# A decoder's expert choices put in ascending order, and part of the experts' outputs gathered during the last pairs of experts

## The chip, the cores and the metric

The kernel runs as one launch on one core of a Trainium2 chip. A core has five engines that run side by side, each with its own stream of instructions: TensorE (PE, matrix products; its weight loads are shown as PEld), VectorE (DVE), ScalarE (ACT), GpSimd (POOL) and SyncE (SP, which here only issues DMAs). They wait for one another by semaphores, and share 16 DMA engines. The metric is the device time of one execution in microseconds, lower is better. The kernel before takes 3460.56 us, the median of 3 runs (3460.08 to 3462.9).

## The reference, cut to what matters

A decoder of two layers works on `x` of 8 batches x 256 tokens x 512 features. Layer 0 has a windowed self-attention, a cross-attention with a layernorm on its result, and a mixture of 64 experts plus a shared expert; layer 1 a Mamba-2 block, a cross-attention and a second feed-forward. Each block's result is added to `x`. The change touches the mixture and its seam to Mamba:

```python
def _L0_ffn_ref(hidden_states, gate_weight, Wg, Wu, Wd, Sg, Su, Sd):
    ...
    logits = x.astype(jnp.float32) @ gate_weight.astype(jnp.float32).T
    scores = jax.nn.softmax(logits, axis=-1)
    group_scores = scores.reshape(T, NG, E // NG).max(axis=-1)
    _, gidx = jax.lax.top_k(group_scores, TG)
    ...
    tmp_scores = jnp.where(smask > 0, scores, 0.0)
    topk_w, topk_i = jax.lax.top_k(tmp_scores, K)
    ...
    slot = flat * C + jnp.minimum(pos, C - 1)
    ...
    out = jnp.einsum('ecm,ehm->ech', jax.nn.silu(g) * u, Wd).reshape(E * C, H)
    yk = out[slot].reshape(T, K, H)
    y = jnp.sum(yk * topk_w[..., None].astype(yk.dtype), axis=1)
    shared = jax.nn.silu(x @ Sg.T) * (x @ Su.T) @ Sd.T
    return (y + shared).reshape(B, S, H)
```

K is 6, E 64, and an expert has C = 192 slots. The sum over a token's six experts is the same in any order of the six, but for rounding. Mamba then reads the layernorm of the new `x`:

```python
    x = x + _L0_ffn_ref(_layernorm(x, axis=-1), L0_ffn_gate_weight, L0_ffn_Wg, L0_ffn_Wu, L0_ffn_Wd, L0_ffn_Sg, L0_ffn_Su, L0_ffn_Sd)
    x = x + _L1_attn_ref(_layernorm(x, axis=-1), L1_attn_in_proj_w, L1_attn_conv_w, L1_attn_conv_b, L1_attn_dt_bias, L1_attn_A_log, L1_attn_D, L1_attn_norm_w, L1_attn_out_proj_w)
```

## The kernel before

`x` stays in SBUF as 16 tiles x0 to x15 of 128 tokens x 512; batch b is x(2b) and x(2b+1). The stages follow one another: attention (0 to 560 us of the profile), cross-attention (560 to 1145), experts (1145 to 1950), Mamba (to about 2370), then the rest of layer 1. All matrix products go through `mm` (L100), all weight loads from DRAM through `load` (L103) and the SP queue into a ring of eight weight tiles `w`.

The cross-attention carries the front of the mixture along with it: in steps of a hand-written table, each batch also gets its layernorm, its routing, its slots, and the shared expert. `l0_choose` takes a batch's 2 x 64 logits per lane, softmaxes them (`sco`), keeps three of eight groups (`gm`), and takes the eight largest (MAX8, L892) with their indices (FIND_INDEX8, L893): weights to `topw`, indices to `topi`, largest weight first. `sel` marks the six chosen (MATCH_REPLACE8, L900). `slot` turns choices into rows of the experts' buffers: three operations on 768 elements (L767 equal, L771 times, L773 sum) pick the position of each choice, and `read[:, k, i]` keeps the row of choice k of x tile i. The shared expert is `hidden(b, m)` for six blocks m (eight matmuls into a PSUM bank, silu on ACT L843 into `act`, a product on DVE L844 into `hT`) and `down`. At the end of the stage a map from slots to tokens is read back from DRAM (L827, tiles `part0`, `part1`) and gives `slots`.

`l0_experts` runs 32 pairs of experts. Per pair POOL gathers three tiles `xg` of 128 rows from `xn_d` by `slots` (L916, an indirect DMA), PE transposes them (`turn`, L926), the copies make `xgT`; per expert three `hidden` steps follow (eight matmuls, silu on ACT L951, product on DVE L952 into `aT`), then `first` (128 of the 192 rows) and, once per pair, `last` (64 rows of both): their results go to the tile `yo` and by the SP queue to `y_d` in DRAM (L962, L977). `first` and `last` of a pair run one step late, `late` holding them.

Mamba starts from the combination of these outputs: `combine(pool, b)` gathers, for each of a batch's two tiles and each k, the rows `read[:, k, i]` of `y_d` into a tile `ye` (indirect DMA issued by POOL, L667, six buffers) and adds it times `topw` to x (DVE, L670). Each gather waits for every write to `y_d`. `normal(b)` is the layernorm of x (L161 to L169, its power on POOL, L153), `turn(b)` PE's transposes of it (L1040, ACT copies to `xnT`, L1041), `steps` and `convolve` the projections, `begin` and `scan` the recurrence in two halves (DVE's `dA` and `tri`, L1104; POOL's `xdt`, L1114), `result` the addition to x. The loop works in rounds: in round b, `turn` works on batch b+2, `normal` on b+3, `combine` on b+4, so four batches of `combine` stand in the program ahead of the first `begin`:

```python
                (turn, 2), (result, 0, 1), (normal, 3), (lambda b: combine(pool, b), 4),
            )
            for b in range(-4, B):
```

The order of instructions on an engine is set by a scheduler from its own estimates, except where `pin` keeps an instruction at its place in the program's order among other pinned ones; all of PE's are pinned, and `in_order` makes `layernorm` and `rsqrt` pin theirs. A pool's tile with a tag has `bufs` buffers (2 if nothing is said), which are handed out in turn; a tile waits until the last reader of the buffer's former tile is done.

Of the kernel before, what the change touches and what calls it, by code (L numbers as in the profile page):

```python
# [18 lines left out]
P = 128  # L19
# [23 lines left out]
    "ident": P, "lt": P, "gt": P, "le": P, "ones": P,  # L43
    "third": HC, "iota": E0, "base": E0,
}
# [23 lines left out]
class Decoder:  # L69
# [578 lines left out]
    def l0_moe(self, outer):  # L648


        nc, a = self.nc, self.a
        xn_d = self.dram.tile([T, D], F32, name="xn_d")
        y_d = self.dram.tile([NSLOT, D], F32, name="y_d")
        keep = outer.enter_context(self.pool("c0k", 1))
        topw = keep.tile([P, NT, 8], F32, name="topw")
        read = keep.tile([P, TOPK, NT], I32, name="read")
        slots = keep.tile([P, NSC], I32, name="slots")
        self.l0_cross(lambda *pools: self.l0_front(*pools, xn_d, topw, read, slots))
        with ExitStack() as ctx:
            self.ps = ctx.enter_context(self.psum("ps"))  # L660
            self.l0_experts(ctx.enter_context(self.pool("c2")), xn_d, slots, y_d)

        def combine(pool, b):
            for i in (2 * b, 2 * b + 1):
                for k in range(TOPK):
                    y = pool.tile([P, D], F32, tag="ye", name="ye", bufs=6)
                    nc.gpsimd.indirect_dma_start(  # L667
                        y, None, y_d, bass.IndirectOffsetOnAxis(ap=read[:, k, i : i + 1], axis=0)
                    )
                    nc.vector.scalar_tensor_tensor(  # L670
                        self.x[i], y, topw[:, i, k : k + 1], self.x[i], ALU.mult, ALU.add
                    )

        return combine

    def l0_front(self, one, pool, bank, xn_d, topw, read, slots):

# [21 lines left out]
        by_lane = lambda m: m.rearrange("(p i) o -> p (i o)", p=P)  # L699
        zero = one.tile([P, NSC], I32, name="zero")  # L700
        nc.vector.memset(zero, 0)
# [28 lines left out]
        def route(b):  # L730
            w = work[b]
            gate = self.small["gate"].rearrange("p (c e) -> p c e", c=HC)
            t = bank()
            lo = t[:, : 2 * E0].rearrange("p (i e) -> p i e", i=2)
            for i in range(2):
                for c in range(HC):
                    self.mm(lo[:, i, :], w["xnT"][:, c, i * P : (i + 1) * P], gate[:, c, :], c == 0, c == HC - 1)
            w["topi"] = topi = pool.tile([P, 2, 8], F32, tag="topi", name="topi")
            w["sel"] = self.l0_choose(pool, lo, topw[:, 2 * b : 2 * b + 2, :], topi)

        def slot(b):
# [11 lines left out]
            for i in range(2):  # L753
# [3 lines left out]
            nc.scalar.copy(pos, t[:, : 2 * E0].rearrange("p (i e) -> p i e", i=2))  # L757
            past = pool.tile([P, 2, E0], F32, tag="past", name="past", bufs=1)
            nc.vector.tensor_scalar(past, pos, CAP - 1.0, float(BAD), ALU.is_ge, ALU.mult)
# [8 lines left out]
                hit, self.iota.unsqueeze(1).unsqueeze(1).to_broadcast(every),  # L768
                w["topi"][:, :, :TOPK].unsqueeze(3).to_broadcast(every), ALU.is_equal,
            )  # L770
# [59 lines left out]
        def hidden(b, m):  # L830
            w = work[b]
            if m == 0:
                w["hT"] = pool.tile([P, n_m, S], F32, tag="hT", name="hT", bufs=1)
            n = rows(m)
            t = bank()
            for h, name in enumerate("gu"):
                for c in range(HC):
                    self.mm(
                        t[:n, h * S : (h + 1) * S], up[name][c // 2][:, c % 2, m * MB : m * MB + n],
                        w["xnT"][:, c, :], c == 0, c == HC - 1,  # L840
                    )
            act = pool.tile([P, S], F32, tag="act", name="act")
            nc.scalar.activation(act[:n], t[:n, :S], AF.Silu)  # L843
            self.pin(nc.vector.tensor_tensor(w["hT"][:n, m, :], act[:n], t[:n, S:], ALU.mult))  # L844
# [12 lines left out]

    def l0_choose(self, pool, logits, topw, topi):

# [35 lines left out]
        t8 = new("t8", 8)  # L895
        nc.vector.tensor_copy(t8, topw)
        nc.vector.memset(t8[:, :, TOPK:], -1.0)
        sel = new("sel", E0)
        for i in range(2):
            nc.vector.match_replace(sel[:, i, :], t8[:, i, :], tmp[:, i, :], -2.0)  # L900
        nc.vector.tensor_scalar(sel, sel, -1.5, None, ALU.is_lt)
        return sel

    def l0_experts(self, pool, xn_d, slots, y_d):

# [34 lines left out]
        def hidden(pair, h, m):  # L940
# [40 lines left out]
        for n in range(3):  # L981
            turn(0, n)
        late = []
        for pair in range(E0 // 2):
            for h in range(2):
                load(pair, h)
                for m in range(3):
                    if h == 0 and pair + 1 < E0 // 2:
                        gather(pair + 1, m)
                    hidden(pair, h, m)  # L990
                    if m == 0:
                        for work in late:
                            work()
                        late = []
                    if (h, m) in ((0, 2), (1, 1), (1, 2)) and pair + 1 < E0 // 2:
                        turn(pair + 1, m if h else 0)
                late = [lambda pair=pair, h=h: first(pair, h)]
                if h == 1:
                    late.append(lambda pair=pair: last(pair))
        for work in late:  # L1000
            work()


    def l1_mamba(self, combine):

# [12 lines left out]
        with ExitStack() as ctx:  # L1018
# [515 lines left out]
def decode(tc, a, out):  # L1534
    with ExitStack() as ctx:
        d = Decoder(ctx, tc, a, out)
        d.load_first()
        with ExitStack() as late:
            d.l0_attention()
            combine = d.l0_moe(late)  # L1540
            d.l1_mamba(combine)
        d.l1_cross()
# [3 lines left out]
def shape_constants():  # L1546
# [17 lines left out]
        "third": np.where(p % HD // 3 == np.arange(HC)[None, :], -1.0, 0.0),  # L1564
        "iota": row(np.arange(E0)), "base": row(np.arange(E0) * CAP),
        "mask": mask, "keep": keep,
# [73 lines left out]
```

## Time and profile before

| what | us |
|---|---|
| median of 3 runs | 3460.56 |
| profiled execution, its own time | 3465.64 |
| profiled execution, its span | 3463.9 |
| PE busy in the span | 3247.0 (94%) |
| DVE busy | 1598.5 (46%) |
| POOL busy | 758.5 (22%) |
| experts: 1145 to 1950, PE busy | 800.71 |
| seam: 1950 to 2000, PE busy | 12.16 |
| first rounds of Mamba: 2000 to 2100, PE busy | 76.09 |
| a steady batch of the cross stage: length, PE busy, DVE busy | 85.5, 82.0, 71.0 |

The profile is of one execution on the chip. Times are in us from the start of the span. A row of instructions gives the line of the kernel, the engine, the operation, the tile written and those read, and the number and length; "[28.60 <-DVE xn L169]" after a row of the timeline says that the engine idled 28.60 us before it, and what ended that. A row of windows gives each engine's busy time in that stretch with the number of its instructions, then the clock granted to TensorE as a share of full speed, the share in which the 16 DMA engines were busy, and the GB/s that they moved. Lengths on POOL are rough, and PE's ends are modelled.

### The profile page before, as it was taken

How to read it: one execution, taken by the hardware profiler on the slowest of the kernel's cores; microseconds unless marked ns; L12 is line 12 of the kernel's file. 1: busy time of each engine (PE TensorE's matmuls, PEld its weight loads, DVE VectorE, ACT ScalarE, POOL GpSimd, SP SyncE). 2: the span in 40 equal slices, each digit the busy share in tenths (PEclk: the TensorE clock that was granted, in tenths of full speed). 3: DMA queues.
4: the chain of work that ended last, by engine and by line, in shares of the span. 5: the costliest groups of instructions: out<-in, count | busy, mean ns of one | idle time of the engine just before them, and what ended most of it. 6: DMA issues, size and time to landing. Idle time of an engine off the chain costs nothing.

```text
span 3463.9 us, 47107 instructions
## 1 busy us (share of the span) xinstructions
PE 3247.0 (94%) x18803; PEld 2114.8 (61%) x18803; DVE 1598.5 (46%) x3784; ACT 998.6 (29%) x1959; POOL 758.5 (22%) x792
## 2 busy tenths in 40 slices
PE   7999878999999899999999578998999899999999
PEld 5666545666666687878787455563444566666665
DVE  4555589888875000000000288655666333333332
ACT  1222223333342122222222133442555322222221
POOL 3222001222235211111110276322121111111111
PEclk9999989999999999999999778997999899999999
DMA  4000010000100677777777743011000000000000
GB/s 175 1 1 1 7 64 16 13 13 13 35 7 21 198 234 236 237 236 242 232 245 224 223 140 91 1 33 50 26 26 17 34 7 6 7 7 1 7 6 13
DMA packets 106812, 272.57 MB, mean 79 GB/s; under 512 B 15136, under 2 KB 23968, under 8 KB 105696
## 3 DMA queue, kind: packets, MB, share of 16 engines
q1 hardware_dynamic: 88128, 219.16, 19.3%
q0 software_dynamic: 18464, 50.40, 5.2%
q8 instruction: 148, 2.42, 0.3%
q14 instruction: 72, 0.59, 0.1%
HBM read 235.81 MB, written 33.70 MB: 78 GB/s over the span
## 4 chain that ended last, share of the span: by engine, by line
PE 67%; DVE 12%; POOL 3%; issue 2%; DMA 2%; ACT 1%; SPq 0%; POOLq 0%; DVEq 0%; ACTq 0%
PE mm L100 18%; PE sc L100 15%; PE out L100 7%; PE w L100 6%; PE s L100 4%; PE a L100 3%; PE b L100 3%; PE sums L100 2%; PE acc L100 2%; PE st L100 2%; DVE e L526 1%; PE pt L926 1%; PE rt L100 1%; POOL ye L667 1%; DVE acc L1066 1%
## 5 line engine op out<-in xcount | busy, mean ns | idle before, releaser
L100 PE MATMUL sc<-xgT,w 128*112 128x192 f32 (+1 forms) x3072 | 529.6, 328 | 0.0
L100 PEld LDWEIGHTS sc<-xgT,w 128*112 128x112 f32 (+1 forms) x3072 | 497.4, 182 | 41.1 <-issue 40.9
L952 DVE TENSOR_TENSOR aT<-act,sc 112x192 f32<-112x192 f32 (+1 forms) x192 | 68.0, 354 | 741.3 <-ACT act L951 741.3
L100 PE MATMUL mm<-xnT,w 128*128 128x256 f32 x1152 | 280.9, 401 | 7.4 <-ACT xnT L252 5.9
L100 PE MATMUL mm<-w,aT 112*128 112x512 f32 (+3 forms) x768 | 262.7, 596 | 0.0
L100 PEld LDWEIGHTS mm<-xnT,w 128*128 128x128 f32 x1152 | 227.2, 201 | 46.2 <-ACT xnT L252 8.2
L100 PE MATMUL w<-xnT,w 128*128 128x256 f32 x1024 | 242.9, 380 | 0.0
L100 PE MATMUL out<-w,mix 128*128 128x512 f32 x512 | 240.4, 592 | 0.0
L1483 DVE TENSOR_TENSOR h<-base,b 128x512 f32<-128x512 f32 x128 | 88.0, 687 | 327.4 <-PE b L100 327.4
L916 POOL DMA_INDIRECT xg<-xn_d,slots x96 | 90.9, 947 | 641.2 <-PE pt L926 634.8
L100 PEld LDWEIGHTS w<-xnT,w 128*128 128x128 f32 x1024 | 192.2, 190 | 61.1 <-issue 40.7
L1487 POOL TENSOR_TENSOR mix<-h 128x256 f32<-128x256 f32 x128 | 93.1, 727 | 610.4 <-DVE h L1485 549.6
L1344 DVE TENSOR_REDUCE m<-s 128x1 f32<-128x512 f32 x256 | 164.6, 685 | 102.3 <-PE s L100 83.5
L153 POOL TENSOR_TENSOR lnr<-lne,c_nhalf 128x1 f32<-128x1 f32 x112 | 66.6, 596 | 645.7 <-DVE lne L151 639.5
L100 PE MATMUL st<-q,k 32*128 32x256 f32 (+1 forms) x1024 | 196.6, 545 | 1.2 <-ACT e L522 1.2
L100 PE MATMUL mm<-mT,w 128*118 128x256 f32 (+1 forms) x768 | 175.2, 388 | 9.8 <-DVE hT L844 9.8
L1293 ACT ACTIVATE e<-st 128x512 f32<-128x512 f32 x256 | 138.9, 595 | 141.9 <-PE st L100 140.2
L951 ACT ACTIVATE act<-sc 112x192 f32<-112x192 f32 (+1 forms) x192 | 63.6, 331 | 402.0 <-PE sc L100 402.0
L100 PEld LDWEIGHTS out<-w,mix 128*128 128x128 f32 x512 | 97.3, 190 | 122.4 <-issue 120.5
L100 PEld LDWEIGHTS mm<-w,aT 112*128 112x128 f32 (+3 forms) x768 | 95.6, 163 | 122.5 <-issue 122.5
L100 PEld LDWEIGHTS mm<-mT,w 128*118 128x118 f32 (+1 forms) x768 | 141.9, 186 | 45.9 <-DVE hT L844 12.1
L100 PE MATMUL s<-k,q 32*128 32x512 f32 x512 | 159.9, 700 | 6.3 <-issue 3.5
(333 smaller groups left out, 5315.1 us busy)
## 6 DMA issues: line engine op xcount, KB each, us to landing
w<-in_Wg SPq DMA_DIRECT2D x64, 704.0 KB, 7.7
w<-in_Wu SPq DMA_DIRECT2D x64, 704.0 KB, 4.6
w<-in_Wd SPq DMA_DIRECT2D x64, 448.0 KB, 6.4
w<-in_Wd SPq DMA_DIRECT2D x64, 256.0 KB, 5.4
y_d<-yo SPq DMA_DIRECT2D x64, 256.0 KB, 3.9
y_d<-yo SPq DMA_DIRECT2D x64, 128.0 KB, 4.1
w<-in_W SPq DMA_DIRECT2D x8, 1024.0 KB, 5.5
x<-in_x SPq DMA_DIRECT2D x16, 256.0 KB, 5.8
```

What stands on the lines that cost most here:

```text
L100: self.pin(self.nc.tensor.matmul(out, lhs, rhs, start=start, stop=stop))
L153: ins = nc.gpsimd.tensor_tensor(r, e, self.nhalf[:, :n], ALU.pow)
L526: self.pin(nc.vector.scalar_tensor_tensor(e, e, 1.0, low, ALU.max, ALU.mult))
L667: nc.gpsimd.indirect_dma_start(y, None, y_d, bass.IndirectOffsetOnAxis(ap=read[:, k, i : i + 1], axis=0))
L916: nc.gpsimd.indirect_dma_start(xg, None, xn_d, bass.IndirectOffsetOnAxis(ap=slots[:, i : i + 1], axis=0))
L926: self.pin(nc.tensor.transpose(t[:, blk], w[n][:, blk], self.ident))
L951: nc.scalar.activation(act[:n_m], ps[:n_m, :CAP], AF.Silu)
L952: nc.vector.tensor_tensor(w["a", h][:n_m, m, :], act[:n_m], ps[:n_m, S : S + CAP], ALU.mult)
L1293: nc.scalar.activation(w["e"][kc][:, j, :], st, AF.Exp, scale=SCALE)
L1344: nc.vector.tensor_reduce(m, sc, AX.X, ALU.max)
L1483: nc.vector.tensor_tensor(both(h), twice(base), both(t), ALU.add)
L1487: nc.gpsimd.tensor_tensor(mix, h[:, :G], h[:, G:], ALU.add)
```

## The change

1. `l0_choose` no longer keeps the largest first. The masked scores go to a tile `gates` (64 per token, kept until the experts are done), the six largest are found as before, `sel` marks them, and the marked indices are then sorted: `sel` times a constant 64 - e (`down`), the eight largest of that (MAX8), and 64 minus those are the indices in ascending order. FIND_INDEX8 and two copies go. So the k-th choice of a token has an index of at most 58 + k.
2. The weights in this order are taken later: `weigh(pool, b)`, three operations on 768 elements for each batch, in the first eight pairs of the experts' stage.
3. In the last two pairs `early` issues three gathers at every `hidden` step, of choices whose experts are all written: k = 0, 1 of x0 to x8 in pair 30, k = 2, 3 of the same tiles in pair 31, 36 of the 96. A gather reads from `known`, the first (59 + k) x 192 rows of `y_d`, and so waits for the writes to these alone. There are twelve buffers `ye` for them; the additions come three steps later, pinned on DVE, and what is left of them after the last pair. The products of `aT` (L952) are pinned too.
4. `combine` has the other 60: four in each of batches 0 to 3, eight in batch 4, twelve in each of batches 5 to 7. `normal(0)` is pinned; after it `hold` copies the indices of x0 to x5 on POOL, and the gathers of batches 1 and 2 read this copy, so they stay behind it.
5. To make room, `act` of the shared expert has one buffer for two, `past` shares a buffer with the scores, and the tile `zero` with `part0`.

In the order of instructions PE's stays as it was. On SP, the read of `part0` moves ahead of a 704 KB weight load at the start of the experts. On POOL, all `xg` gathers come ahead of all `ye` gathers. ACT has two table loads more, and one copy of `xgT` at the start of the experts goes from ACT to DVE.

```diff
@@ -652,28 +652,67 @@
         xn_d = self.dram.tile([T, D], F32, name="xn_d")
         y_d = self.dram.tile([NSLOT, D], F32, name="y_d")
         keep = outer.enter_context(self.pool("c0k", 1))
-        topw = keep.tile([P, NT, 8], F32, name="topw")
+        inner = ExitStack()
+        chosen = inner.enter_context(self.pool("c0g", 1))
+        gates = chosen.tile([P, NT, E0], F32, name="gates")
+        topi = chosen.tile([P, NT, 8], F32, name="topi")
+        topw = keep.tile([P, NT, TOPK], F32, name="topw")
         read = keep.tile([P, TOPK, NT], I32, name="read")
         slots = keep.tile([P, NSC], I32, name="slots")
-        self.l0_cross(lambda *pools: self.l0_front(*pools, xn_d, topw, read, slots))
+        self.l0_cross(lambda *pools: self.l0_front(*pools, xn_d, gates, topi, read, slots))
+
+        todo = [(i, k) for i in range(NT) for k in range(TOPK)]
+
+        def fetch(pool, i, k, bufs=6, at=read):
+            y = pool.tile([P, D], F32, tag="ye", name="ye", bufs=bufs)
+            known = y_d[: (E0 - TOPK + k + 1) * CAP, :]
+            nc.gpsimd.indirect_dma_start(
+                y, None, known, bass.IndirectOffsetOnAxis(ap=at[:, k, i : i + 1], axis=0)
+            )
+            return y
+
+        def add(i, k, y):
+            return nc.vector.scalar_tensor_tensor(self.x[i], y, topw[:, i, k : k + 1], self.x[i], ALU.mult, ALU.add)
+
+        def early(pool, done, n):
+
+            got = [(i, k) for i, k in todo if E0 - TOPK + k < done][:n]
+            for ik in got:
+                todo.remove(ik)
+            got = [(i, k, fetch(pool, i, k, 12)) for i, k in got]
+            return [lambda g=g: self.pin(add(*g)) for g in got]
+
+        def weigh(pool, b):
+
+            two = slice(2 * b, 2 * b + 2)
+            every = [P, 2, TOPK, E0]
+            hit = pool.tile(every, F32, tag="hit", name="hit", bufs=1)
+            nc.vector.tensor_tensor(
+                hit, self.iota.unsqueeze(1).unsqueeze(1).to_broadcast(every),
+                topi[:, two, :TOPK].unsqueeze(3).to_broadcast(every), ALU.is_equal,
+            )
+            nc.vector.tensor_tensor(hit, hit, gates[:, two, :].unsqueeze(2).to_broadcast(every), ALU.mult)
+            nc.vector.tensor_reduce(topw[:, two, :], hit, AX.X, ALU.add)
+
         with ExitStack() as ctx:
             self.ps = ctx.enter_context(self.psum("ps"))
-            self.l0_experts(ctx.enter_context(self.pool("c2")), xn_d, slots, y_d)
+            self.l0_experts(ctx.enter_context(self.pool("c2")), xn_d, slots, y_d, weigh, early)
+        inner.close()
+
+        held = []
+
+        def hold(pool):
+
+            held.append(pool.tile([P, TOPK, 6], I32, name="held"))
+            self.pin(nc.gpsimd.tensor_copy(held[0], read[:, :, :6]))
 
         def combine(pool, b):
-            for i in (2 * b, 2 * b + 1):
-                for k in range(TOPK):
-                    y = pool.tile([P, D], F32, tag="ye", name="ye", bufs=6)
-                    nc.gpsimd.indirect_dma_start(
-                        y, None, y_d, bass.IndirectOffsetOnAxis(ap=read[:, k, i : i + 1], axis=0)
-                    )
-                    nc.vector.scalar_tensor_tensor(
-                        self.x[i], y, topw[:, i, k : k + 1], self.x[i], ALU.mult, ALU.add
-                    )
-
-        return combine
-
-    def l0_front(self, one, pool, bank, xn_d, topw, read, slots):
+            for i, k in [t for t in todo if t[0] // 2 == b]:
+                add(i, k, fetch(pool, i, k, at=held[0] if held and b in (1, 2) else read))
+
+        return combine, hold
+
+    def l0_front(self, one, pool, bank, xn_d, gates, topi, read, slots):
 
 
         nc, a = self.nc, self.a
...
@@ -697,7 +736,7 @@
 
         maps = [self.dram.tile([NSLOT, 1], I32, name=f"map{k}_d") for k in range(2)]
         by_lane = lambda m: m.rearrange("(p i) o -> p (i o)", p=P)
-        zero = one.tile([P, NSC], I32, name="zero")
+        zero = pool.tile([P, NSC], I32, tag="part0", name="zero", bufs=1)
         nc.vector.memset(zero, 0)
         for m in maps:
             self.pin(nc.sync.dma_start(by_lane(m), zero))
...
@@ -755,7 +794,7 @@
                 nc.vector.tensor_tensor(cum, cum, sel, ALU.add)
                 nc.vector.scalar_tensor_tensor(late, sel, token[:, 2 * b + i : 2 * b + i + 1], late, ALU.mult, ALU.max)
             nc.scalar.copy(pos, t[:, : 2 * E0].rearrange("p (i e) -> p i e", i=2))
-            past = pool.tile([P, 2, E0], F32, tag="past", name="past", bufs=1)
+            past = pool.tile([P, 2, E0], F32, tag="sco", name="past", bufs=1)
             nc.vector.tensor_scalar(past, pos, CAP - 1.0, float(BAD), ALU.is_ge, ALU.mult)
             nc.vector.scalar_tensor_tensor(
                 pos, pos, CAP - 1.0, self.base.unsqueeze(1).to_broadcast([P, 2, E0]), ALU.min, ALU.add
...
@@ -839,7 +878,7 @@
                         t[:n, h * S : (h + 1) * S], up[name][c // 2][:, c % 2, m * MB : m * MB + n],
                         w["xnT"][:, c, :], c == 0, c == HC - 1,
                     )
-            act = pool.tile([P, S], F32, tag="act", name="act")
+            act = pool.tile([P, S], F32, tag="act", name="act", bufs=1)
             nc.scalar.activation(act[:n], t[:n, :S], AF.Silu)
             self.pin(nc.vector.tensor_tensor(w["hT"][:n, m, :], act[:n], t[:n, S:], ALU.mult))
 
...
@@ -883,25 +922,27 @@
         for i in range(2):
             nc.vector.match_replace(gm[:, i, :], g8[:, i, :], gs[:, i, :], -2.0)
         nc.vector.tensor_scalar(gm, gm, -1.5, None, ALU.is_lt)
-        tmp = new("tmp", E0)
         nc.vector.tensor_tensor(
-            groups(tmp), groups(sco), gm.unsqueeze(3).to_broadcast([P, 2, NG, E0 // NG]), ALU.mult
+            groups(gates), groups(sco), gm.unsqueeze(3).to_broadcast([P, 2, NG, E0 // NG]), ALU.mult
         )
-        ti = new("ti", 8, U32)
+        t8 = new("t8", 8)
         for i in range(2):
-            nc.vector.max(topw[:, i, :], tmp[:, i, :])
-            nc.vector.max_index(ti[:, i, :], topw[:, i, :], tmp[:, i, :])
-        nc.vector.tensor_copy(topi, ti)
-        t8 = new("t8", 8)
-        nc.vector.tensor_copy(t8, topw)
+            nc.vector.max(t8[:, i, :], gates[:, i, :])
         nc.vector.memset(t8[:, :, TOPK:], -1.0)
         sel = new("sel", E0)
         for i in range(2):
-            nc.vector.match_replace(sel[:, i, :], t8[:, i, :], tmp[:, i, :], -2.0)
+            nc.vector.match_replace(sel[:, i, :], t8[:, i, :], gates[:, i, :], -2.0)
         nc.vector.tensor_scalar(sel, sel, -1.5, None, ALU.is_lt)
+
+        order = new("sco", E0)
+        nc.vector.tensor_tensor(order, sel, self.down.unsqueeze(1).to_broadcast(wide), ALU.mult)
+        for i in range(2):
+            nc.vector.max(t8[:, i, :], order[:, i, :])
+        nc.vector.tensor_scalar(topi, t8, -1.0, float(E0), ALU.mult, ALU.add)
         return sel
 
-    def l0_experts(self, pool, xn_d, slots, y_d):
+    def l0_experts(self, pool, xn_d, slots, y_d, weigh, early):
+
 
 
         nc, a = self.nc, self.a
...
@@ -949,7 +990,7 @@
                     )
             act = pool.tile([P, CAP], F32, tag="act", name="act", bufs=3)
             nc.scalar.activation(act[:n_m], ps[:n_m, :CAP], AF.Silu)
-            nc.vector.tensor_tensor(w["a", h][:n_m, m, :], act[:n_m], ps[:n_m, S : S + CAP], ALU.mult)
+            self.pin(nc.vector.tensor_tensor(w["a", h][:n_m, m, :], act[:n_m], ps[:n_m, S : S + CAP], ALU.mult))
 
         def first(pair, h):
             w = state[pair]
...
@@ -980,8 +1021,10 @@
             gather(0, n)
         for n in range(3):
             turn(0, n)
-        late = []
+        late, adds, done = [], [], 0
         for pair in range(E0 // 2):
+            if pair < B:
+                weigh(pool, pair)
             for h in range(2):
                 load(pair, h)
                 for m in range(3):
...
@@ -992,16 +1035,22 @@
                         for work in late:
                             work()
                         late = []
+                        if h == 0:
+                            done = 2 * pair
+
+                    adds.append(early(pool, done, 3) if done >= E0 - 4 else [])
+                    for work in adds.pop(0) if len(adds) > 3 else []:
+                        work()
                     if (h, m) in ((0, 2), (1, 1), (1, 2)) and pair + 1 < E0 // 2:
                         turn(pair + 1, m if h else 0)
                 late = [lambda pair=pair, h=h: first(pair, h)]
                 if h == 1:
                     late.append(lambda pair=pair: last(pair))
-        for work in late:
+        for work in late + sum(adds, []):
             work()
 
 
-    def l1_mamba(self, combine):
+    def l1_mamba(self, combine, hold):
 
 
 
...
@@ -1185,7 +1234,13 @@
             for b in range(-4, B):
                 for work, ahead, *more in round_:
                     if 0 <= b + ahead < B:
-                        work(b + ahead, *more)
+                        if work is normal and b + ahead == 0:
+                            self.in_order = True
+                            normal(0)
+                            self.in_order = False
+                            hold(one)
+                        else:
+                            work(b + ahead, *more)
 
     def softplus(self, pool, ps):
 
```

More of the change, by code (lines that the diff above doesn't have):

```diff
@@ L43 @@
     "ident": P, "lt": P, "gt": P, "le": P, "ones": P,
-    "third": HC, "iota": E0, "base": E0,
+    "third": HC, "iota": E0, "base": E0, "down": E0,
 }
@@ L737, in route @@
                     self.mm(lo[:, i, :], w["xnT"][:, c, i * P : (i + 1) * P], gate[:, c, :], c == 0, c == HC - 1)
-            w["topi"] = topi = pool.tile([P, 2, 8], F32, tag="topi", name="topi")
-            w["sel"] = self.l0_choose(pool, lo, topw[:, 2 * b : 2 * b + 2, :], topi)
+            two = slice(2 * b, 2 * b + 2)
+            w["sel"] = self.l0_choose(pool, lo, gates[:, two, :], topi[:, two, :])
         def slot(b):
@@ L768, in slot @@
                 hit, self.iota.unsqueeze(1).unsqueeze(1).to_broadcast(every),
-                w["topi"][:, :, :TOPK].unsqueeze(3).to_broadcast(every), ALU.is_equal,
+                topi[:, 2 * b : 2 * b + 2, :TOPK].unsqueeze(3).to_broadcast(every), ALU.is_equal,
             )
@@ L856, in l0_front, with l0_choose @@
         }
-    def l0_choose(self, pool, logits, topw, topi):
+    def l0_choose(self, pool, logits, gates, topi):
         nc = self.nc
@@ L1539, in decode @@
             d.l0_attention()
-            combine = d.l0_moe(late)
-            d.l1_mamba(combine)
+            d.l1_mamba(*d.l0_moe(late))
         d.l1_cross()
@@ L1564, in shape_constants @@
         "third": np.where(p % HD // 3 == np.arange(HC)[None, :], -1.0, 0.0),
-        "iota": row(np.arange(E0)), "base": row(np.arange(E0) * CAP),
+        "iota": row(np.arange(E0)), "base": row(np.arange(E0) * CAP), "down": row(E0 - np.arange(E0)),
         "mask": mask, "keep": keep,
```

## The prediction, made before the changed kernel ran

> **What bounds the kernel now.** I read the windows by stage first, then PE's and POOL's waits at the seam between experts and mamba, then the timeline there, the tiles `ye` and `xg`, and 5 us windows of the last pairs.
>
> ```profile
> core 0: us, PE busy (x) PEld busy (x) DVE busy (x) ACT busy (x) POOL busy (x), PEclk, DMA share, GB/s
> 1145.00:1950.00 805.00, 800.71 (x4218) 635.47 (x4220) 68.02 (x192) 175.54 (x383) 88.94 (x94) 0.99 0.74 235
> 1950.00:2000.00 50.00, 12.16 (x49) 9.47 (x45) 20.97 (x37) 3.46 (x6) 30.88 (x32) 0.56 0.69 204
> 2000.00:2100.00 100.00, 76.09 (x277) 49.84 (x276) 81.82 (x177) 32.72 (x77) 77.71 (x75) 0.80 0.47 132
> 2100.00:2300.00 200.00, 178.81 (x705) 115.94 (x704) 134.94 (x315) 80.65 (x214) 82.91 (x76) 0.92 0.09 27
> ```
>
> Experts (1145 to 1950) are bound by PE; DVE is busy 8% there. In the next 50 us PE is busy 12, and in the 100 us after DVE and POOL are as busy as PE. The waits (total, times, longest) say on what:
>
> ```profile
> PE pt L1040 <- DVE xn L169: 37.8, 2, 28.6
> PE sc L100 <- DVE tri L1104: 11.0, 6, 6.3
> POOL ye L667 <- DMA w<-in_W: 87.3, 1, 87.3
> ```
>
> Mamba's first transposes wait for the layernorm of x0 and x1, which waits for their twelve gathers and adds, and POOL's first gather waits for a DMA. The timeline (start, busy):
>
> ```profile
> 1950.69 1.03 PE L100 MATMUL mm<-w,aT 112*64 112x512 f32 x4
> ...
> 1961.27 0.94 POOL L667 DMA_INDIRECT ye<-y_d,read  x1 [87.26 <-DMA w<-in_W]
> 1962.52 0.95 POOL L667 DMA_INDIRECT ye<-y_d,read  x1 [0.30 <-issue]
> ...
> 1980.32 1.11 PE L1040 MATMUL pt<-c_const,xn 128*128 128x128 f32 x4 [28.60 <-DVE xn L169]
> ...
> 1990.68 1.12 PE L1040 MATMUL pt<-c_const,xn 128*128 128x128 f32 x4 [9.24 <-DVE xn L169]
> ```
>
> The releaser named is a 1 MB W1 load; what the gather needs are the last y_d writes, issued at 1952.41 on the same queue behind the W1 loads of 1945.15, 1946.45 and 1951.75, and landed at about 1960.2. So the seam is 1951.7 to 1990.7: 9.6 us for the last results, 29.4 for gathers and adds. Rows of `ye`, then the landing of `xg`, a gather of the same size issued while weights load:
>
> ```profile
> L667 POOL DMA_INDIRECT ye<-y_d,read x96: 942/1022/1465, 1961.3 to 2140.4; - x96
> L670 DVE SCALAR_TENSOR_TENSOR x<-ye,topw,x x96: 690/745/3842, 1964.6 to 2151.3; 128x512 f32<-128x512 f32 x96
> DMA to landing us min/median/max: 3.3/3.7/4.5
> ```
> ```profile
> DMA to landing us min/median/max: 3.3/6.4/8.6
> ```
>
> A gather takes POOL 1.02 + 0.30 of issue = 1.32 us, an add 0.745 on DVE. Mamba's rounds, from the copy of one xnT to the next: 68 us (2015 to 2083), 48, 47.7, then 38.7, 40.4 and 39.7. Free of gathers a round is about 39.6; the first three lose 28.4 + 8.4 + 8.1 = 45 us.
>
> **The change, part by part.** The time is summed against the profiled run (span 3463.9, its own time 3465.64, 5.1 above the median of 3460.56); I apply the differences to the median.
>
> *Early gathers.* 36 of 96 (k=0,1 of x0 to x8 in pair 30, k=2,3 in pair 31) with their adds go into the last two pairs. Of batch 0 four gathers are left of twelve. POOL: pair 30's 18 take 18 x 1.32 = 24 us of a 25 us pair, and POOL is otherwise idle, its `xg` gathers having ended at 1873. Pair 31's must wait until last(30) has landed, 1936.9, so POOL is done at about 1936.9 + 23.8 = 1961. The DMAs:
>
> ```profile
> 1915.00:1920.00 5.00, 5.00 (x27) 4.02 (x26) 0.33 (x1) 1.17 (x3) 0.00 (x0) 1.00 0.42 160
> 1935.00:1940.00 5.00, 5.00 (x27) 4.24 (x26) 0.71 (x2) 0.66 (x2) 0.00 (x0) 1.00 1.06 385
> 1955.00:1960.00 5.00, 0.00 (x0) 0.00 (x0) 0.00 (x0) 0.00 (x0) 0.00 (x0) 0.50 0.99 351
> ```
>
> Over 1910 to 1960 the shares average about 0.74: 13 us idle. A gather moves 262 KB, 0.7 us at the 385 GB/s of the full window at 1935, and 36 take 25 us. Some 12 us are left over at 1960. In order of issue that delays the last y_d writes from 1960.2 to between 1966 and 1969, and batch 0's first gather to 1968.8 at worst; four gathers, 3.7 landing, adds and a layernorm then give x1's xn at 1979.7 in place of 1990.6: **-11 us**. Ends: 0, if the adds or writes are later still, and -18, if nothing is delayed (first gather at 1962, x1's xn near 1973).
>
> What is queued behind the waits: the adds are pinned on DVE three steps after their gathers, in front of the next aT mult (L952), for which PE's first() waits. In pair 30 a gather has 8 to 12 us and is not late. In pair 31 the second group is issued at 1941 to 1945 and lands at 1949 to 1951 with the worst `xg` landing; its three adds (2.2 us) hold aT(31,1,2), which PE needs at 1948. PE then stops for some 5 us, and the last results leave as much later. That is one of the reasons for 1966 to 1969, so it is in the -11 and not added to it.
>
> *Rounds.* Up to batch 0's first xdt (L1114) 20 gathers are left on POOL for 42, in the two marks after it 2 + 18 for 7 + 25, then 2 + 18 for 2 + 20. Round 0 has 12 fewer: 12 x 1.32 = 15.8 us of POOL's 50.4 busy, 12 x 0.745 = 8.9 of DVE's 58.8. PE's gaps there are DVE's (`tri`); DVE from dA to `tri` loses 7. I take **-11** (ends -7 and -15.8). Round 1 keeps 20 of 22: **-2**. Round 2's six gathers are a backlog of POOL, 6 x 1.32 = 7.9 us, that would be gone: **-7** of its 8.1. Together -20 (-28 to -8). The normal(0) now pinned lets the two L153 pows follow batch 0's gathers; before they were at 1979.03 and 1989.41, each behind gathers already. `hold` copies 128x36 words on POOL, between 0.1 (MEMSET of 128x18, 0.19 for two) and 0.73 us (a 128x256 TENSOR_TENSOR), under the wait for the landings.
>
> *Cross stage.* Choosing: out go 2 x (0.219 + 0.078) for FIND_INDEX8 and 0.201 + 0.205 for two copies, 1.00 us; in come 0.292 + 2 x 0.218 + 0.174 = 0.90. Nothing. But `act` has one buffer, so silu (L843) of hidden m+1 must wait for the mult (L844) of m. Now the two are back to back on DVE:
>
> ```profile
> 796.24 0.74 DVE L844 TENSOR_TENSOR hT<-act,mm 118x256 f32<-118x256 f32 x2
> 796.70 6.28 PEld L100 LDWEIGHTS mm<-mT,w 128*118 128x118 f32 x22 [3.30 <-DVE hT L844]
> ```
>
> After, the second stands behind L527, L579 and nan_clean (L178 to L181), which end at 802.5, where PE takes its PSUM bank from 801.94: 0.7 us in each of about 6 steady batches. In 13 of 24 pairs the next silu started before the mult ended, and each such pair pays at most one silu, 0.38. So 6 x 0.7 = 4: **+4** (ends -1 and +10, the latter if PE's gap of 2.48 there, with 8 matmuls at 0.43 us in place of 0.215 behind it, comes once more in four batches: 4 x (0.7 + 1.7)). By the Trainium skill ("TensorE: Matmul & The Clock Gate", Part 1) the clock falls only after an idle window of about 3.4 us; by it the doubled spacing would not be bought by so short a gap and the upper end would be +4; this trace shows the slower matmuls after 2.48 us.
>
> *Start of the experts.* 24 `weigh` operations of 768 elements, 0.95 us each by rows L767 to L773, 22.8 us in all, on a DVE that idles 92%; eight of them stand before the first aT and one `xgT` copy is on DVE: **+1** (0 to 3, the last if three of them hold an aT). Two more ACT table loads lie in the same slack. The `part0` read goes ahead of a 704 KB load that landed at 1141.19 and held `slots` at 1141.45: **-1.5** (-3 to 0).
>
> Sum: -11 - 20 + 4 + 1 - 1.5 = -27.5, so **3433 us**.
>
> **Rivals.** *Nothing is delayed by the gathers* (20%). For it: 5 us windows at 0.42 to 0.63, and landings of 3.3. Against: the windows at 1935, 1950 and 1955 are full. Then the start gains 17, the rounds 24, and the cross stage costs 1: 3460.6 - 17 - 24 + 1 - 1.5 = 3419.
>
> *The gathers take the last pair's time* (17%). For it: 8.6 us landings, DMA full from 1950 to 1960, adds pinned ahead of aT. Then PE's stop in pair 31 is some 15 us (both later groups late by another landing), the start gains nothing, the rounds 15: 3460.6 - 15 + 4 = 3449. The Trainium skill ("DMA: Bandwidth & Descriptors", Issuing engines are not separate DMA queues) says that transfers of all issuers run on the same 16 engines and interleave; by it the 12 us of backlog would fall on the y_d writes in full, 1960 to 1972, and the start would gain 7 in place of 11: 3437. The landing of `xg` at 8.6 against 3.3 agrees.
>
> *Slower: the single `act` buffer* (9%). For it: DVE is busy 71 of 85.5 us of a cross batch, PE 82, so a late hidden is not made up. If the 13 conflicts turn into 24 and each stops PE 0.9 us plus the 0.85 of a cold restart (8 matmuls lose 1.7, in half of them), 24 x 1.75 = 42 against a gain of 31.5: 3460.6 + 10 = 3471. It decides from 1.3 us a pair on. Against: PE's waits for L844 are 8.4 us in all today.
>
> *It does not do what it says*: the order of instructions has 36 gathers moved and PE's order unchanged; the gathers left are 60. I give this nothing beside the other cases.
>
> **Numbers.** Forecast 3433: 54%; 3419: 20%; 3449: 17%; 3471: 9%. The forecast's own ends, all costs at their bad or good end together, are far wider than likely; with half of each way it runs 3421 to 3446. The 80% range takes in 3419 and 3449 with some margin: 3411 to 3457. 0.2%, about 7 us, is what a measurement here can tell from no change: faster than 3453.6 holds the first two cases and two thirds and more of the third, 0.86; within, 0.06; slower, 0.08.
>
> **What would show it.** Right: 36 gathers before 1955, batch 0's first at 1962 to 1970, x1's transposes near 1980, round 0 at 57 and round 2 at 41, a PE wait of 3 to 8 us on aT at the last first(). If landings in pair 31 stay under 5 us, the second case holds; if PE stops there over 10 us, the third; if a cross batch takes over 87 us for 85.5, the fourth. The sum is wrong if round 0 stays near 68: then neither gathers nor adds set it.

## The result, and the profile after

The changed kernel takes 3451.19 us (median of 9 runs, 3445.19 to 3456.94); the kernel before, on the same chips, 3460.08 (9 runs, 3458.05 to 3465.47). The ratio is 0.9974, 95% interval [0.9963, 0.9984]: 8.9 us faster, where 27.5 was forecast. The time lies in the range, on the side of the third case (3449). The profiled execution took 3448.02 us (span 3446.2), 3.2 under its median, and that of before 5.6 over its own; of the 17.6 us between the two, 8.7 are such scatter.

The windows by stage after, same columns as before:

```profile
1145.00:1950.00 805.00, 793.32 (x4157) 626.57 (x4158) 94.12 (x223) 175.36 (x380) 105.86 (x111) 0.99 0.74 236
1950.00:2000.00 50.00, 25.30 (x98) 16.76 (x97) 24.01 (x41) 5.42 (x10) 29.89 (x32) 0.67 0.79 284
2000.00:2100.00 100.00, 81.22 (x329) 55.21 (x327) 85.31 (x204) 39.14 (x94) 72.01 (x71) 0.91 0.38 110
2100.00:2300.00 200.00, 184.37 (x746) 119.43 (x747) 131.77 (x304) 82.23 (x212) 78.19 (x70) 0.95 0.07 20
```

In the experts PE is now busy 793.3 of 805, not 800.7: something stops it there. PE's waits from 1950 to 2300:

```profile
PE pt L1089 <- DVE xn L169: 21.3, 2, 20.2
...
PE sc L100 <- DVE tri L1153: 5.0, 5, 2.6
```

The waits at the seam and in the first rounds have shrunk as meant (37.8 to 21.3, 11.0 to 5.0). PE's instructions stand in the same order in both kernels, so the n-th can be laid beside the n-th. How much later it starts than before:

| PE's instruction, at its time in the kernel before | 560 | 1100 | 1106 | 1160 | 1900 | 1945 | 1951 | 1992 | 2083 | 2297 | 3400 |
|---|---|---|---|---|---|---|---|---|---|---|---|
| later by, us | -3.8 | -3.8 | +0.6 | -0.3 | -0.3 | +13.4 | +19.8 | +3.3 | -14.8 | -17.0 | -17.6 |

Attention, which the change doesn't touch, is 3.8 us quicker in this execution. Cross stage and start of the experts cost 3.5, all of it after 1100. Then PE loses 13.7 us between 1900 and 1945, in pair 30, and some 6 more at the end of pair 31; the seam and the rounds win 36.9 back. The timeline of pair 30 (start, busy):

```profile
1919.29 2.76 PE L100 MATMUL sc<-xgT,w 128*112 128x192 f32 x16
...
1920.17 0.75 DVE L675 SCALAR_TENSOR_TENSOR x<-ye,topw,x 128x512 f32<-128x512 f32 x1 [5.58 <-DMA ye<-y_d,read]
...
1923.18 2.20 DVE L675 SCALAR_TENSOR_TENSOR x<-ye,topw,x 128x512 f32<-128x512 f32 x3 [0.22 <-issue]
1925.45 0.19 PEld L100 LDWEIGHTS sc<-xgT,w 128*128 128x128 f32 x1 [0.83 <-issue]
1926.15 0.32 PE L100 MATMUL sc<-xgT,w 128*128 128x192 f32 x1 [1.09 <-issue]
...
1934.57 0.33 SPq L103 DMA_DIRECT2D w<-in_Wu  x1
...
1936.75 0.33 ACT L992 ACTIVATE act<-sc 112x192 f32<-112x192 f32 x1 [14.26 <-PE mm L100]
1936.98 0.58 ACT L968 COPY xgT<-pt 128x512 f32<-128x512 f32 x1
1937.11 0.35 DVE L993 TENSOR_TENSOR aT<-act,sc 112x192 f32<-112x192 f32 x1 [11.73 <-ACT act L992]
...
1937.52 1.22 PE L100 MATMUL mm<-w,aT 112*128 112x512 f32 x1 [1.73 <-DVE aT L993]
```

The matmuls of the first row are those of the last hidden step of pair 30; by the trace they end at 1922.05. In the kernel before, ACT's silu starts 0.04 us after such a group. Here it starts at 1936.75, 14.7 us after. SP's load of Wu, which waits for the first half of the same matmuls, leaves at 1934.57. Silu, the copy of a transposed tile done at 1922.5 and the next step's silu then follow one another within 0.7 us: what was held was not PE's work but its signals, and they were let go together. (PE's ends are modelled, but the trace also records the updates of the semaphore that ACT and SP wait for: those of the two halves of this group come at 1934.56 and 1936.73, though later matmuls had already started at 1922.54.) PE itself first ran on, then crept at one instruction each 0.7 us, though the weights that it needed had landed by 1919.75, and then waited for the aT that hung on that silu. Its instructions came no later than usual as far as the trace shows: the 16 KB instruction packet at 1916.8 took 1.16 us, the one at 1916.1 in the kernel before 1.10. No add is in front of that aT for more than 2.2 us. The gathers' packets ran from 1916 to 1936.

### The profile page after: what moved, and what is told of

The parts are those of the page before. It is cut to its first block, busy times and chain, and to the rows that moved or that the text cites. A ratio compares the mean times of both kernels' runs of the same rounds, so it can differ in the third digit from the quotient of the medians.

```text
span 3446.2 us, 47114 instructions
## 1 busy us (share of the span) xinstructions
PE 3247.0 (94%) x18803; PEld 2110.2 (61%) x18803; DVE 1618.0 (47%) x3793; ACT 1001.0 (29%) x1960; POOL 759.6 (22%) x793
## 4 chain that ended last, share of the span: by engine, by line
PE 70%; DVE 11%; issue 2%; POOL 2%; DMA 2%; ACT 1%; POOLq 0%; SPq 0%; DVEq 0%; ACTq 0%
PE mm L100 20%; PE sc L100 15%; PE out L100 7%; PE w L100 6%; PE s L100 4%; PE a L100 3%; PE b L100 3%; PE st L100 2%; PE sums L100 2%; PE acc L100 2%; PE pt L967 1%; PE rt L100 1%; PE acc L543 1%; DVE acc L1115 1%; DVE e L526 1%
## 5 line engine op out<-in xcount | busy, mean ns | idle before, releaser
L100 PE MATMUL mm<-w,aT 112*128 112x512 f32 (+3 forms) x768 | 270.8, 611 | 7.6 <-issue 4.9
```

The costliest lines, as they stand in the source:

```text
L100: self.pin(self.nc.tensor.matmul(out, lhs, rhs, start=start, stop=stop))
```

## The experiments

*Terms.* "Loss in pair 30" is what PE falls behind the kernel before between its instructions at 1900 and 1945, "start" from 1900 to 1992 (x1's transposes are done; all losses in the pairs are in it), "rounds" from 1992 to 2297. Times in us.

| kernel | early gathers, buffers | median | loss in pair 30 | start | rounds |
|---|---|---|---|---|---|
| changed | 36, 12 | 3451.2 | 13.7 | +3.5 | -20.3 |
| no_early | 0 | 3465.1 | 0.0 | -11.8 | +6.5 |
| pair30 | 18, 12 | 3457.5 | 13.7 | +0.6 | -1.3 |
| pair31 | 18, 12 | 3450.7 | 2.7 | -9.1 | -7.0 |
| adds_after | 12, 12 | 3452.1 | 2.8 | -11.4 | -1.7 |
| one_three | 12, 3 | 3452.9 | 0.0 | -17.4 | +3.1 |
| one_three_act | 12, 3 | 3453.7 | 0.0 | -16.8 | +6.2 |
| two_six | 24, 6 | 3441.0 | 0.0 | -12.9 | -10.6 |
| three_six | 36, 6 | 3436.1 | 1.5 | -7.5 | -20.3 |
| three_nine | 36, 9 | 3450.1 | 3.1 | +2.3 | -20.3 |

**First: what is the early gathers' doing, and where?** One line of `l0_experts` was changed in each; in adds_after the two lines that issue adds inside the pairs were left out too.

```diff
-                    adds.append(early(pool, done, 3) if done >= E0 - 4 else [])
+no_early            adds.append([])
+pair30              adds.append(early(pool, done, 3) if done == E0 - 4 else [])
+pair31              adds.append(early(pool, E0 - 4, 3) if done == E0 - 2 else [])
+adds_after          adds.append(early(pool, done, 3) if done == E0 - 4 and m + 3 * h < 4 else [])
```

> No gathers before the end of the experts: all 96 stay in combine; choices, weigh, hold, the pinned layernorm and the smaller buffers stay. Theory G (the early gathers alone make both the gain and the loss): 3460 us, within 4 of the kernel before, and no PE stop in pair 30. Rival R (the pinned layernorm and the order of POOL's gathers make a good part of the gain in the first rounds): 3452 or less, round 0 at 60 us or less for 68.

3465.05 us (10 runs), ratio 1.001 [1.0001, 1.002]; no stop in pair 30. Theory G holds in the main: without the early gathers the rest of the change wins nothing; it costs 4.7 us against the 3460.3 of the kernel before on that chip, a little more than the 4 allowed. The part that stays, with the pinned layernorm in it, does bring x1's transposes 11.8 us forward, but the rounds give 6.5 of it back; that the same gathers and adds then stand in front of the next batches is a likely reason, not tested.

> Early gathers in pair 30 alone (18, their adds three steps later as before), none in pair 31. Theory G: the 13.4 us that PE lost from 1923 to 1940 are lost again, the 5.8 us at the last first() are not; half of the gain in the rounds is left: 3453 us. Rival T (the two lots of gathers disturb each other only together): PE loses under 5 us and the time is 3443.

3457.5 us (10 runs), 0.9989 [0.998, 0.9999]. The loss is there in full, 13.7: the two lots need not come together, theory G. The gain is under half of what was expected.

> The 18 gathers of k=0 and k=1 issued in pair 31 in place of 30, nothing in pair 30. Theory G (a gather for every 1.25 us slows PE wherever it runs beside hidden steps): PE loses 10 to 14 us in pair 31, 3457 us. Rival P (it depends on the place: in pair 30 PE's releases of weight tiles and the last loads come on top; in pair 31 no weights of experts are loaded): PE loses 2 to 6 us there, 3447 us.

3450.66 us (6 runs), 0.9974 [0.9961, 0.9986]; 2.7 lost, as rival P had it. But the loss is again in pair 30: twelve gathers leave POOL from 1913 on, as soon as pair 29's results have landed, since POOL has nothing else to wait for; only the buffers stop the thirteenth. Where the program issues these gathers doesn't set when they run; their data and their buffers do. The run is one of twelve gathers, not of a place.

> 12 gathers in the first four steps of pair 30, none later, and their adds only after the last pair, so nothing is pinned on DVE ahead of an aT. Theory G: PE still loses some 9 us (12 of 18 gathers), ACT wakes late after PE, 3457 us. Rival D (the adds ahead of aT on DVE cause the stop): PE loses under 1 us there, and the time is 3449.

3452.1 us (10 runs), 0.9973 [0.9964, 0.9983]; 2.8 lost, ACT's silu 6.5 late, with no add on DVE: between the two expectations (9 and under 1). So signals are late without any add; twelve gathers in a row cost far less than eighteen, not in proportion as theory G had it.

**Second: the suspected cost by itself, mid-stage.** To no_early, 18 transfers were added into tiles that nothing reads (12 or 2 buffers; in extra_plain the last line was a plain transfer of 128 rows).

```diff
+                    for q in range(3 if pair == 16 else 0):
+                        y = pool.tile([P, D], F32, tag="ye", name="ye", bufs=12)
+                        i = 9 * h + 3 * m + q
+                        nc.gpsimd.indirect_dma_start(y, None, xn_d, bass.IndirectOffsetOnAxis(ap=slots[:, i : i + 1], axis=0))
```

> The kernel of no_early with 18 more gathers of 128 rows (from xn_d by slots, into tiles that nothing reads) in pair 16, twelve buffers, no adds: the suspected cost by itself, in the middle of the experts. Theory S (while a bunch of gathers runs on the DMA engines, PE's signals to ACT and SP are held back): ACT's silu comes 6 to 15 us after its matmuls there, and PE loses 5 to 14 us; 3470 to 3479 us. Rival E (it needs the end of the stage, where y_d is written and mamba's weights are loaded): under 2 us lost, 3466.

> The same 18 gathers with two buffers in place of twelve, so at most two are under way. Theory S with a bunch as the condition: silu within 0.5 us of its matmuls, PE loses under 2 us, 3466 us. Rival N (the number of gathers decides, not how many are under way): 5 to 14 us lost as with twelve buffers.

> 18 plain transfers of the same size (256 KB, rows of 2 KB, issued by POOL) in place of the gathers, twelve buffers. If it is the traffic on the DMA engines: signals as late as with the gathers, 5 to 14 us lost. If it is the gathers' own way of running: silu within 0.5 us, under 2 us lost, 3466 us.

One execution each: 3466.92, 3468.68 and 3459.82 us; PE lost 0.0 in all three. Nothing ties these transfers to pair 16, so they ran at the start of the experts. Every kernel with the change has one step there whose silu is 1.6 us late, behind another ACT instruction. Besides that, with twelve buffers silu came up to 2.6 us late in five steps, and that one step was 3.6 late; with two buffers 1.1 in one step; with plain transfers never over 0.3. The sign of theory S is there, its price isn't, although POOL issued 24 gathers there, the stage's own among them, without a pause over 0.5 us. Why the same transfers cost so little at this place is not shown, and the next runs had to decide in pair 30 itself.

**Third: fewer buffers, fewer a step.** Rate and buffers of the early gathers were changed (n a step, bufs).

```diff
-            got = [(i, k, fetch(pool, i, k, 12)) for i, k in got]
+            got = [(i, k, fetch(pool, i, k, bufs)) for i, k in got]
...
-                    adds.append(early(pool, done, 3) if done >= E0 - 4 else [])
+                    adds.append(early(pool, done, n) if done >= E0 - 4 else [])
```

> The changed kernel with one early gather a step in place of three and three buffers in place of twelve: 12 gathers in all, at most three under way. Theory S: PE loses under 1.5 us in pair 30 and the time is 3444 to 3448, faster than the changed kernel with a third of its early gathers. Rival D (the adds pinned on DVE ahead of aT are the cost): PE still waits 4 us or more for aT in pairs 30 and 31, 3452.

3452.93 us (10 runs), 0.9977 [0.9968, 0.9987]. No loss in any pair and no late silu, as theory S said; but `combine` is left with 84 gathers in place of 60, the rounds win nothing, and the expected time was too hopeful by 5 us.

> The changed kernel with six buffers for the early gathers in place of twelve; still 36 of them, three a step, but at most six under way. Theory B (signals are held while a bunch of more than some six gathers is under way): PE loses under 4 us in pair 30 in place of 13.4, ACT's silu there comes under 3 us late, and the time is 3440 to 3446. Rival D (adds and gathers wait for one another through the buffers, and DVE holds aT): PE loses 8 us or more in the last pairs, 3450 or more.

3436.12 us (4 runs), 0.9927 [0.9911, 0.9944]: faster than both kernels, with the same 36 gathers. In pair 30 PE loses 1.5, and no silu is over 0.7 late. PE's waits from 1905 to 2300 show what is left:

```profile
PE pt L1089 <- DVE xn L169: 20.6, 2, 19.4
PE mm L100 <- DVE aT L993: 5.2, 2, 4.0
```

The second line is pair 31: adds that wait for landings hold aT on DVE. With the stops before and after it this costs 8 us.

The price goes as theory B had it, but its reason does not hold: the number under way is the same. Counted by the packets on POOL's queue (64 of 4 KB to a gather), at most six gathers are between issue and last packet in pair 30 with twelve buffers, and at most six with six. What six buffers change is the row. With twelve, POOL issues all 18 at one each 1.25 us, as here,

```profile
1918.71 0.95 POOL L669 DMA_INDIRECT ye<-y_d,read  x1 [0.30 <-issue]
```

and in three_six it stops for a buffer after the sixth:

```profile
1918.94 0.95 POOL L669 DMA_INDIRECT ye<-y_d,read  x1 [0.30 <-issue]
1922.78 0.95 POOL L669 DMA_INDIRECT ye<-y_d,read  x1 [2.89 <-DMA ye<-y_d,read]
```

> Two early gathers a step and six buffers: 24 of them. Theory B: PE loses under 3 us in the last pairs, round 0 gets two thirds of its gain, 3441 to 3447 us. Rival D: 6 us or more lost, 3450.

3440.98 us (4 runs), 0.9948 [0.9931, 0.9964]; 0.0 lost in pair 30, some 4 in pair 31. That is the price that theory B forecast; here POOL pauses 2.0 us after the sixth gather. Against three_six, with 12 gathers more, the medians are 4.9 us apart, but the two profiled executions only 0.6, so four runs each leave open what the 12 are worth.

> one_three with the last pair's five writes of y_d issued by ACT in place of SP, so that they don't stand behind the 1 MB loads of W1 on SP's queue. If that queue is what holds them: batch 0's first gather 3 to 4 us earlier after the end of the experts (10.2 us in one_three from PE's last product to POOL's first gather of batch 0), 3449 us. If the DMA engines are shared whatever the queue: under 1 us, 3453 us.

3453.7 us (10 runs), 0.9977 [0.9968, 0.9987]. From PE's last product to batch 0's first gather it takes 8.4 us, 8.6 in one_three, so SP's queue is not what holds them. The last write lands 8.6 us after its issue on ACT's queue and 7.4 on SP's; that the loads of W1 on the same DMA engines are the reason is likely, not tested. (The 10.2 in the expectation was too long a reading.)

**Fourth: what the hold hangs on.** gather30 and plain30 have no_early's 96 gathers in `combine`, and 18 more transfers of rows of y_d at the steps of pair 30, twelve buffers, read by nothing.

```diff
+gather30    nc.gpsimd.indirect_dma_start(y, None, known, bass.IndirectOffsetOnAxis(ap=read[:, k, i : i + 1], axis=0))
+plain30     nc.gpsimd.dma_start(y, y_d[at : at + P, :])
```

> The kernel of no_early with the 18 gathers of pair 30 (same rows of y_d, twelve buffers) into tiles that nothing reads: no adds, and all 96 gathers still in combine. Theory B: PE loses 10 to 14 us in pair 30 and ACT's silu comes 10 us or more after its matmuls, with no add on DVE anywhere near. Rival D (the adds are needed for the stop): under 4 us.

> The same with 18 plain transfers of 128 rows of y_d issued by POOL at the same place, twelve buffers. If the traffic on the DMA engines holds the signals: 10 us or more as with the gathers. If it takes gathers: silu within 0.5 us of its matmuls; PE loses under 4 us, what the weight loads are late by.

One execution each: 3484.18 and 3466.16 us. PE loses 14.1 and 0.0 in pair 30. What ACT waited for, 1905 to 1950, and a window of 5 us, gather30:

```profile
ACT act L998 <- PE mm L100: 14.2, 1, 14.2
```
```profile
1930.00:1935.00 5.00, 2.96 (x15) 2.62 (x16) 0.00 (x0) 0.00 (x0) 3.78 (x5) 0.99 0.75 206
1935.00:1940.00 5.00, 2.50 (x3) 0.64 (x3) 0.00 (x0) 0.00 (x0) 3.78 (x5) 0.50 0.73 221
```

and plain30:

```profile
ACT act L996 <- PE sc L100: 23.5, 11, 2.3
```
```profile
1930.00:1935.00 5.00, 5.00 (x30) 3.61 (x27) 0.00 (x0) 0.88 (x2) 0.69 (x1) 1.00 1.04 342
1935.00:1940.00 5.00, 5.00 (x31) 4.90 (x31) 0.71 (x2) 0.46 (x3) 0.00 (x0) 1.00 1.05 387
```

With gathers the DMA engines are less busy (0.73 to 0.75, 206 to 221 GB/s) and PE all but stands, from 30 instructions to 15 and 3; with plain transfers they are full and PE runs on. There is no add in either. So neither the adds nor the bytes on the DMA engines hold the signals; it takes the gathers. In plain30 up to eight transfers are under way, more than the five of gather30, so the number under way doesn't do it either. A gather also keeps POOL busy for 0.95 us, a plain transfer for 0.55 with pauses between; whether the gathers' packets or POOL's issuing holds the signals, these two runs don't separate.

> The changed kernel with nine buffers, between six (1.5 us lost in pair 30) and twelve (13.4). If the hold grows with the number under way: 4 to 9 us lost in pair 30, 3441 to 3446 us. If it needs more than nine: under 2 us lost, 3436 us or less.

3450.1 us (7 runs), 0.9967 [0.9956, 0.9979]; 3.1 lost in pair 30, silu up to 5.2 late: the loss lies between six buffers and twelve, if under the 4 to 9 expected. The number under way is at most five here, so again it isn't that; POOL issues some of them later, up to 2.3 us apart for 1.25. That the time is no better than with twelve comes from pair 31, where PE loses 15 us more, 8.5 of it for an aT behind adds:

```profile
PE mm L100 <- DVE aT L993: 8.5, 1, 8.5
```

## Why the prediction was wrong

- *The step that failed:* the price to PE of the gathers in pair 30, which the sum put at nothing. The forecast counted a gather as POOL time, DMA share and an add, found room for each ("POOL is otherwise idle", "In pair 30 a gather has 8 to 12 us and is not late"), and stopped there. The adds are not what stopped PE. While 18 gathers followed one another without a pause, PE's signals to ACT and SP came up to 14.7 us late, and PE lost 13.7. With six buffers, which break the row, that step costs 1.5, and three_six measures 3436 where 3433 was forecast for twelve. That the rest of the sum comes out so well is in part luck, as the next points show.
- *Start:* -11 forecast, +3.5 found; the difference, 14.5, is the loss in pair 30 but for 0.8. But the -11 was credited to the eight gathers that batch 0 no longer has, and no_early, which has them all, shows -11.8 at the same place: most of this gain comes with the rest of the change. From PE's 1951 to 1992 the changed kernel wins 16.6 and no_early 11.8. The stop in pair 31 came as worked out (5 forecast, some 6 found). That POOL's gathers would wait for last(30) before the second lot came true too, at 1951 in place of 1937, late by that loss.
- *Rounds:* -20 forecast, -20.3 found, in three kernels with 36 early gathers alike. How it divides among the rounds was wrong: 18 of it fall in round 0 (11 forecast), and round 2 wins 2.5 (7 forecast). PE's waits for `tri` fell from 11.0 to 5.0; why round 0 wins more than they do is not shown. And no_early loses 6.5 in the rounds, so that the early gathers win about 27 there.
- *Cross stage and the start of the experts:* +4, +1 and -1.5 forecast together, +3.5 found, by luck. The +4 was the price of the single `act` buffer, six conflicts of 0.7 us. Up to 1100 the cross stage loses 0.0, and PE's waits for hT went from 9.8 to 7.5 us: the buffer costs nothing. Of the other fourteen kernels, with the same cross stage, nine show 3.6 to 4.6, four -2.2 to +0.6 and one 7.6; what makes the difference is told below.
- *The third case* (gathers take the last pair's time, 3449) met the time by another road: it put a stop of 15 us in pair 31 and on DVE. three_nine shows that this road exists as well.
- *The DMA backlog:* the 12 us left over were to delay the last writes of y_d by 6 to 9 us. They don't: the last one lands 7.5 us after its issue, 7.3 in the kernel before. A gather's packets do take 0.7 us where several wait, as at 1918 to 1920, but after that they come at POOL's pace, one gather for 1.25 us (206 to 221 GB/s in gather30), and leave no backlog. That transfers of all issuers run on the same 16 engines and interleave (the Trainium skill, "DMA: Bandwidth & Descriptors", Issuing engines are not separate DMA queues) agrees with one_three_act: moving the last writes to ACT's queue changed 0.2 us in the wait for batch 0's first gather.

## What to carry to other kernels

A row of gathers that is issued under another stage can have a price beyond its queue time: here 18 in a row without a pause cost 13.7 us, and fewer buffers (six, not twelve) broke the row and most of the cost. Test it with a copy of the gathers that nothing reads. POOL, with nothing else to do, started the moved gathers as soon as their data and buffers allowed, wherever the program put them, so the buffers were the throttle. When two kernels issue PE's work in the same order, lay the n-th instruction beside the n-th: one table shows where each microsecond went.

## What the runs showed that was not expected

- *Late signals.* ACT's silu after its matmuls: 0.04 us as a rule; 14.7 to 16.1 late with a row of 18 gathers and twelve buffers, 6.4 to 6.5 with twelve gathers, 5.2 with nine buffers, at most 1.6 with six, none with three, none with plain transfers of the same bytes (all in pairs 30 and 31). With rows of 12 or 18 and twelve buffers the held signals end within 1.4 us of the gathers' last packet; with nine buffers they come while packets still run. What holds them, no run shows; it stays open. The number under way is not the condition (six or fewer wherever gathers ran in pair 30, eight in plain30), and the length of the row is not the whole of it, since 24 gathers in a row at the start of the experts (extra12) cost PE nothing.
- *The clock after a short stop.* In the last cross batch PE stops 1.4 to 1.5 us for L169 in every kernel with the change. In the changed kernel's profile the clock then falls to 0.50 for 6.8 us, as in nine other kernels; in adds_after, after the same stop, it doesn't, nor in three others:

```profile
1102.00:1106.00 4.00, 4.00 (x12) 3.16 (x12) 2.33 (x14) 0.70 (x4) 2.61 (x3) 0.50 0.01 0
```
```profile
1103.00:1107.00 4.00, 4.00 (x20) 3.39 (x19) 2.82 (x20) 1.21 (x5) 1.93 (x2) 1.00 0.01 0
```

12 matmuls in 4 us for 20: some 3.3 us of the 5.4 between the cross stage that costs 3.5 in one execution and the one that gains 1.9 in the other. In three_nine, the 7.6 above, PE stops twice, 1.3 and 1.5 us, and the clock is down for 10.2 us. In the kernel before there is no such stop. The Trainium skill ("TensorE: Matmul & The Clock Gate", Part 1) asks for an idle window of about 3.4 us and notes that the window runs freely and results vary from run to run; the variation agrees with these rows, the length doesn't.
